# Reordered work at both ends of a 32-sequence graph-attention kernel: statistics, reciprocals, adds and a weight combination

## The chip, the cores and the metric

The kernel runs on one core of one Trainium2 chip. The metric is the device time of one execution in microseconds (us), as the median of several executions; before the change it is 3678.03 us (3 runs, 3677.95 to 3679.01; the profiled run took 3678.18). The profile takes one execution apart. In it PE is TensorE's matmuls, PEld its weight loads, DVE is VectorE, ACT ScalarE, POOL GpSimd and SP SyncE, which starts transfers. L389 is line 389 of the kernel that was profiled. A PSUM tile (psum.tile in the code) is a buffer into which matmuls write their results. "Half clock" is a stretch in which the profile gives TensorE's granted clock as 0.50, as from 217 to 223 us before the change. The change adds some ten lines, so one statement has different line numbers before and after; the tile names stay.

## The reference, cut to what matters

Two residual layers act on x of 32 sequences x 512 rows x 512 features, with one adjacency matrix of 512 x 512 for all.

```python
# layer 0: masked attention, 8 heads of 64
h = jnp.maximum(_layernorm(x), 0.0)
q, k, v = h @ Wq + bq, h @ Wk + bk, h @ Wv + bv          # split into heads
scores = q @ k.T / sqrt(64) + (1.0 - adj) * -1e9
x = x + (softmax(scores) @ v) @ Wo + bo
# layer 1: graph attention, one head
h = jnp.maximum(_layernorm(x), 0.0)
g = h @ W;  s1, s2 = g @ a1, g @ a2
e = leaky_relu(s1[:, None] + s2[None, :], 0.2) * adj
x = x + elu(softmax(e) @ g + beta * g)
```

## The kernel before

It runs in steps. Step b works on layer 0 of sequence b, on the output projection of sequence b-1 and on layer 1 of sequence b-2. Each step is a string of parts in the order in which they are issued. The instructions of one engine run in the order in which they are issued; engines wait for one another only where data demand it. Small VectorE jobs ("later") stand in queues: each is due after so many us of TensorE work, and is issued where the issuing code finds it due, or where somebody needs it. So a number in a table of due times decides an order on VectorE.

```python
GAP = (12.0, 14.0, 28.0, 24.0)                       # when the reciprocals of a head pair are due
GAPS = {0: (14.0, 1.0, 4.0, 24.0), 1: (12.0, 12.0, 2.0, 24.0)}
# ...
        for k in range(T):
            mask(k)                                  # additive mask of the scores, four tiles
            dve(1.9)
        for t in range(T):
            later("bad", 30.0, 200.0, 1.35, lambda t=t: other(t))   # is adj 0/1? tiles sq, bad
# ...
    def finish(b, j, st):                            # softmax denominators of one pair of heads
        need("rd")
        pd = psum.tile([P, N], F32, name=f"pd_{b}_{j}", tag="pd")
        # ... matmuls of the sums of e with ones into pd ...
        for k in range(2):                           # two reciprocals rd, then o * rd on GpSimd
            later("rd", 0.0, gap(b, (j + 1) % NP) + 3.0, 1.7, lambda k=k: divide(k))

    def residual(b, st, i, tag="x1", bufs=3):        # x + c_row, the start of the residual
        # ... load ...
            for t in range(n):
                nc.gpsimd.tensor_tensor(r[:, t, :], r[:, t, :], c_row, op=ALU.add)
# ...
    def final(b, t, st):                             # one output tile: matmuls py, then
        # ...
        nc.scalar.activation(y, p, AF.Exp, scale=r)
        nc.vector.tensor_scalar(y, y, 1.0, -1.0, op0=ALU.min, op1=ALU.add)
        nc.vector.scalar_tensor_tensor(y, p, r, y, op0=ALU.mult, op1=ALU.max)
        dve(1.9)
        nc.gpsimd.tensor_tensor(y, y, x1_of(st, t), op=ALU.add)
        nc.sync.dma_start(out[b, ts(t, P), :], y)
# ...
        def W():                                     # output projection of sequence b-1 ...
            need("wa")
            fourth(b - 1, "uT", prev["oT"])
            run(out_proj(b - 1, prev))               # ... whose last pieces queue statistics
            if b == B:
                run_all(("hn", b - 1))               # norm and the two dots of each row tile
# ...
        order = {
            0: "0.V1.NH2c.3wK.Q", 1: "0.VUrR1.W2.NH3K.Q", B - 1: "0.VDU1.rRG2.W3.t", B: "0yrR.zUWDGY",
            B + 1: "DGJY",
        }.get(b, "0.VDU1.G2.rYNRWH3.KQ")
# ...
        combine(nc.vector, wk, ak)                   # at the start: five combinations of wk's blocks
        turn(0, states[0])
        t1 = first_combo(0, "tT", states[0]["h"][0], nc.vector)     # the difference tT
```

The letters: a digit is the scores (matmuls ps, tiles e) of that head pair and the values (po) of the pair before; "." its denominators (pd); V, K, Q the projections of layer 0; r and R the two halves of the residual; U the combinations oT and uT of the attention's output; W the output projection; D the "diagonal" of layer 1 (row sums pe, then beta on the diagonal of the attention tiles at); G the matmuls pg; Y the output tiles (py, then y); y and z output tiles of sequence b-3. A projection is made in seven products of halves instead of eight; its PSUM tiles are x, qz and y, with the weight's letter behind (x_k, qz_q, y_w). Every sequence's dot products pass through DRAM as a row (s) before the tiles at can be made.

## Time and profile before

| what | value |
|---|---|
| time, median | 3678.03 us |
| span of the profiled execution | 3676.4 us |
| TensorE busy | 3606.2 us, 98% of the span |
| TensorE not busy | 70.2 us |
| its waits from 3520 us to the end | 34.8 us |
| its waits from 300 to 3450 us | 9.4 us in 28 pieces |

TensorE is the bound; what can be won is its idle time, and the slow matmuls behind long idle times. The three views to read are the busy line of the page, the list of what TensorE waited for, cut by time, and the timeline around each wait. The prediction shows the lines.

### The profile page before, as it was taken

What the parts mean: (1) busy time and instruction counts of PE and PEld (TensorE: products, weight loads), DVE (VectorE), ACT (ScalarE), POOL (GpSimd) and SP (SyncE); (2) the same over time, 40 slices, a digit from 0 to 9 for tenths busy, and PEclk for the clock granted to TensorE, in tenths of its full rate; (3) what the DMA queues carried; (4) which work ended last, traced back from release to release, by engine and by line L of the source; (5) the groups of instructions that cost most, each with busy time, mean ns of one, the idle gap of its engine ahead of it and who ended that gap; (6) DMA issues with size and microseconds to landing.
All of it is one profiled execution on the core that took longest, in us unless ns stands there. A gap on an engine that the chain in (4) does not pass through costs nothing. (4 is left out here: it accounts for less than half of the span.)

```text
span 3676.4 us, 58866 instructions
## 1 busy us (share of the span) xinstructions
PE 3606.2 (98%) x24310; PEld 1875.1 (51%) x24310; DVE 2802.5 (76%) x4119; ACT 1398.2 (38%) x2086; POOL 1147.1 (31%) x965
## 2 busy tenths in 40 slices
PE   9999999999999999999999999999999999999986
PEld 5545554555554555545555545555455555455532
DVE  6977777787777877777877778777778777787783
ACT  3433334334333433343333334333434343343331
POOL 5423333223333222332233332323332333323241
PEclk9999999999999999999999999999999999999998
DMA  3001111101111011111011110011110111100100
GB/s 130 18 7 35 38 38 35 33 9 38 38 38 35 10 32 38 38 35 38 4 38 38 38 35 14 28 38 38 35 38 4 38 38 38 35 18 24 32 27 27
DMA packets 71074, 120.58 MB, mean 33 GB/s; under 512 B 11856, under 2 KB 15952, under 8 KB 70800
## 3 DMA queue, kind: packets, MB, share of 16 engines
q1 hardware_dynamic: 69216, 114.91, 9.9%
q8 instruction: 193, 3.16, 0.4%
q10 hardware_dynamic: 1376, 1.57, 0.1%
q14 instruction: 81, 0.66, 0.1%
q0 software_dynamic: 208, 0.27, 0.0%
HBM read 83.11 MB, written 33.62 MB: 32 GB/s over the span
## 5 line engine op out<-in xcount | busy, mean ns | idle before, releaser
L620 POOL TENSOR_TENSOR oT<-oT,rd 128x512 f32<-128x512 f32 x128 | 167.2, 1306 | 1527.1 <-DVE rd L613 1524.5
L567 ACT ACTIVATE e<-e 128x1024 f32<-128x1024 f32 x512 | 541.0, 1057 | 196.0 <-DVE e L552 160.0
L552 DVE TENSOR_TENSOR e<-ps,nmT 128x1024 f32<-128x1024 f32 x384 | 455.1, 1213 | 101.9 <-PE ps L542 101.8
L542 PE MATMUL ps<-qT,kT 64*128 64x512 f32 x2048 | 483.4, 606 | 12.7 <-DVE e L552 12.7
L590 PE MATMUL po<-e,v 128*64 128x512 f32 x2048 | 463.1, 593 | 0.0
L51 PE MATMUL pg<-at,hn 128*64 128x512 f32 x2048 | 449.7, 598 | 13.2 <-DVE dmax L775 13.2
L51 PE MATMUL py<-w,gT 128*64 128x512 f32 x2048 | 447.4, 595 | 0.1
L613 DVE RECIPROCAL rd<-pd 128x256 f32<-128x256 f32 x256 | 435.0, 1729 | 0.0
L804 POOL TENSOR_TENSOR y<-y,x 128x512 f32<-128x512 f32 x128 | 193.2, 1509 | 544.9 <-DVE y L802 489.9
L542 PEld LDWEIGHTS ps<-qT,kT 64*128 64x128 f32 x2048 | 184.2, 186 | 309.4 <-issue 214.9
L564 DVE TENSOR_TENSOR es<-es,e 128x1024 f32<-128x1024 f32 x254 | 316.6, 1246 | 13.2 <-ACT e L567 0.6
L51 PEld LDWEIGHTS pg<-at,hn 128*64 128x64 f32 x2048 | 148.9, 138 | 307.5 <-issue 307.5
L51 PEld LDWEIGHTS py<-w,gT 128*64 128x64 f32 x2048 | 148.1, 138 | 293.9 <-issue 292.3
L590 PEld LDWEIGHTS po<-e,v 128*64 128x64 f32 x2048 | 157.8, 138 | 235.1 <-issue 225.4
L598 ACT COPY oT<-po 128x512 f32<-128x512 f32 x128 | 73.8, 576 | 388.2 <-PE po L590 388.2
L714 DVE CUSTOM_DVE_ANT_0 scr<-hn,wa_r 128x512 f32<-128x512 f32 x256 | 169.9, 719 | 49.0 <-ACT hn L701 49.0
L619 ACT ACTIVATE rj<-rd 128x512 bf16<-128x512 f32 x128 | 80.7, 630 | 327.5 <-DVE rd L613 327.4
L741 ACT ACTIVATE at<-at 128x512 f32<-128x512 f32 x128 | 80.4, 628 | 286.3 <-DVE at L737 286.3
L800 ACT ACTIVATE y<-py,rd 128x512 f32<-128x512 f32 x128 | 87.6, 685 | 261.2 <-PE py L51 253.0
L564 DVE TENSOR_TENSOR es<-e,e 128x1024 f32<-128x1024 f32 x127 | 180.9, 1424 | 0.7 <-PE pd L605 0.7
L639 POOL TENSOR_TENSOR x<-x,c_row 128x512 f32<-128x512 f32 x128 | 176.9, 1403 | 0.0
L321 POOL TENSOR_TENSOR rs<-rs,mhalf 128x2 f32<-128x2 f32 (+1 forms) x97 | 78.7, 811 | 306.9 <-DVE rs L320 305.8
(189 smaller groups left out, 5726.5 us busy)
## 6 DMA issues: line engine op xcount, KB each, us to landing
x<-in_x_dram SPq DMA_DIRECT2D x128, 256.0 KB, 3.0
out_dram<-y SPq DMA_DIRECT2D x128, 256.0 KB, 2.1
x<-in_x_dram SPq DMA_DIRECT2D x63, 512.0 KB, 4.2
s<-row_s SPq DMA_DIRECT2D x32, 256.0 KB, 4.2
adj<-in_adj_dram SPq DMA_DIRECT2D x4, 256.0 KB, 7.1
w<-in_L_gnn_W_dram SPq DMA_DIRECT2D x1, 1024.0 KB, 7.9
wk<-in_L_gnn_Wk_dram ACTq DMA_DIRECT2D x3, 256.0 KB, 8.9
wq<-in_L_gnn_Wq_dram SPq DMA_DIRECT2D x3, 256.0 KB, 7.6
```

The costliest lines, as they stand in the source:

```text
L51: nc.tensor.matmul(out[s : s + HD], lhsT[:, s : s + HD], rhs, start=start, stop=stop, skip_group_check=onto)
L542: nc.tensor.matmul(ps[s], st["kT"][j][rows, ts(k, P)], st["qT"][j][rows, :], start=True, stop=True)
L552: nc.vector.tensor_tensor(e, p, nmT[:, k, :].unsqueeze(1).to_broadcast([P, 2, N]), op=ALU.add)
L564: (nc.gpsimd if early else nc.vector).tensor_tensor(es, one, e, op=ALU.add)
L567: nc.scalar.activation(e, e, AF.Exp)
L590: nc.tensor.matmul(po[s * HD : (s + 1) * HD, :], v[k // 2][:, k % 2, (2 * j + s) * HD : (2 * j + s + 1) * HD], e[k][:, s, :], start=k == 0 ...
L613: nc.vector.reciprocal(rd[:, ts(k, H)], pd[:, ts(k, H)])
L620: nc.gpsimd.tensor_tensor(o, o, rd, op=ALU.mult)
L639: nc.gpsimd.tensor_tensor(r[:, t, :], r[:, t, :], c_row, op=ALU.add)
L714: nc.vector.tensor_tensor_reduce(scr, st["hn"][t], r, 1.0, 0.0, op0=ALU.mult, op1=ALU.add, accum_out=st["s12"][:, g, t : t + 1],)
L800: nc.scalar.activation(y, p, AF.Exp, scale=r)
L804: nc.gpsimd.tensor_tensor(y, y, x1_of(st, t), op=ALU.add)
```

## The change

Its intent is to shorten TensorE's waits at both ends, where there is no other sequence's work to fill them. Its parts: (1) only the first of wk's five combinations stays ahead of the difference tT, for which the second group of matmuls, qz_k, waits; (2) two masks are queued; (3) the adjacency checks (sq, bad) are due at 60 instead of 30; (4) the reciprocals of sequence 1's third pair are due at 14 instead of 24, and the last sequence gets due times of its own; (5) in the last step VectorE, not GpSimd, adds c_row to the residual and the residual to the outputs of sequence 30; (6) the statistics of sequence 31 come after the diagonal of sequence 30.

```diff
-GAPS = {0: (14.0, 1.0, 4.0, 24.0), 1: (12.0, 12.0, 2.0, 24.0)}
+GAPS = {0: (14.0, 1.0, 4.0, 24.0), 1: (12.0, 12.0, 2.0, 14.0)}
+LAST_GAPS = (3.0, 14.0, 12.0, 3.0)
 ...
         for k in range(T):
-            mask(k)
-            dve(1.9)
+            if k < 2:
+                mask(k)
+                dve(1.9)
+            else:
+                later("nm", 0.0, 5.0, 1.9, lambda k=k: mask(k))
         for t in range(T):
-            later("bad", 30.0, 200.0, 1.35, lambda t=t: other(t))
+            later("bad", 60.0, 200.0, 1.35, lambda t=t: other(t))
 ...                                   (combine is split into combine_first and combine_rest)
-        return GAPS.get(b, GAP)[j]
+        return (LAST_GAPS if b == B - 1 else GAPS.get(b, GAP))[j]
 ...
+        eng = nc.vector if b == B - 1 else nc.gpsimd
 ...
-                nc.gpsimd.tensor_tensor(r[:, t, :], r[:, t, :], c_row, op=ALU.add)
+                eng.tensor_tensor(r[:, t, :], r[:, t, :], c_row, op=ALU.add)
 ...
-        nc.gpsimd.tensor_tensor(y, y, x1_of(st, t), op=ALU.add)
+        (nc.vector if b == B - 2 else nc.gpsimd).tensor_tensor(y, y, x1_of(st, t), op=ALU.add)
 ...
-            if b == B:
-                run_all(("hn", b - 1))
 ...
-            "t": T1, "J": judge,
+            "t": T1, "n": lambda: run_all(("hn", b - 1)), "J": judge,
 ...
-            0: "0.V1.NH2c.3wK.Q", 1: "0.VUrR1.W2.NH3K.Q", B - 1: "0.VDU1.rRG2.W3.t", B: "0yrR.zUWDGY",
+            0: "0.V1.NH2c.3wK.Q", 1: "0.VUrR1.W2.NH3K.Q", B - 1: "0.VDU1.rRG2.W3.t", B: "0yrR.zUWDnGY",
 ...
-        combine(nc.vector, wk, ak)
+        combine_first(nc.vector, wk, ak)
         turn(0, states[0])
         t1 = first_combo(0, "tT", states[0]["h"][0], nc.vector)
+        combine_rest(nc.vector, wk, ak)
 ...
+        need("nm")
         for b in range(B + 2):
```

## The prediction

> **What bounds the kernel now.** I read the page first: TensorE is busy 98% of the span, at full clock in every slice, the last excepted.
>
> ```profile
> PE 3606.2 (98%) x24310; PEld 1875.1 (51%) x24310; DVE 2802.5 (76%) x4119; ACT 1398.2 (38%) x2086; POOL 1147.1 (31%) x965
> ...
> PE   9999999999999999999999999999999999999986
> ```
>
> So 70.2 us of the span (3676.4 - 3606.2) is all that a change which touches no matmul can win; part of it is mere issue time. The second view, TensorE's waits by window, says where they lie: from 400 to 3300 us only 8.7 us, in 26 pieces of at most 0.3. The middle is one long row of matmuls, so what the start gains reaches the end whole. From 3520 us on there are 34.8 us of waits; four of the six rows (what was waited for; us in total, times, longest):
>
> ```profile
> PE pg L51 <- DVE dmax L775: 13.2, 2, 11.1
> PE pe L51 <- DVE as L748: 10.6, 1, 10.6
> PE pd L605 <- DVE rd L613: 4.9, 1, 4.9
> PE y_w L51 <- POOL uT L379: 3.7, 1, 3.7
> ```
>
> The first 300 us hold some 16 us more. The third view, the timeline (start, duration, engine, line, operation, count, idle before), gives the three waits of the start that the change aims at:
>
> ```profile
> 18.51 0.69 DVE L373 TENSOR_TENSOR tT<-hT 128x512 f32<-128x512 f32 x1
> ...
> 19.34 1.95 PE L51 MATMUL qz_k<-tT,wk 128*64 128x256 f32 x16 [1.54 <-DVE tT L373]
> ...
> 81.62 1.13 PE L542 MATMUL ps<-qT,kT 64*128 64x512 f32 x4 [1.54 <-DVE e L552]
> ...
> 219.06 1.98 PE L605 MATMUL pd<-es,ones 128*64 128x512 f32 x4 [5.49 <-DVE rd L613]
> 220.82 3.03 PE L51 MATMUL x_v<-wv,hT 128*64 128x256 f32 x16
> 223.68 1.90 PE L51 MATMUL qz_v<-wv,hT 128*64 128x256 f32 x16
> ```
>
> The last three lines show a cost that no wait list has: after the idle 5.49 us the four pd take 1.98 us (1.08 elsewhere) and the 16 x_v 3.03 (1.90). From 219.06 to 223.68 is 4.62 us for 0.91 + 1.73 = 2.64 us of work, so 1.98 us is lost behind the wait. The waits of 4.86, 11.14 and 10.60 us at the end are followed by the same slow matmuls (for the second, 64 pg in 16.29 us against 13.90); those of 1.54 and 3.74 us are not.
>
> **What the skill says.** "TensorE: Matmul & The Clock Gate", section "What's actually happening", gives half clock after about 3.4 us of idleness and full clock after about 3.4 us of work. The trace agrees: the edge lies between 3.74 and 4.86 us, and a crossing loses 2.0 to 2.9 us. "SBUF — State Buffer", section "Who interferes with whom", says that GpSimd and a VectorE instruction with two SBUF inputs take an exclusive lock, one wholly blocking the other. The trace agrees: beside GpSimd's adds a dot product on VectorE takes 1.74 us, alone 0.69:
>
> ```profile
> 3551.67 6.29 POOL L639 TENSOR_TENSOR x<-x,c_row 128x512 f32<-128x512 f32 x4
> ...
> 3555.10 1.74 DVE L714 CUSTOM_DVE_ANT_0 scr<-hn,wa_r 128x512 f32<-128x512 f32 x1
> ...
> 3560.12 0.68 DVE L714 CUSTOM_DVE_ANT_0 scr<-hn,wa_r 128x512 f32<-128x512 f32 x1
> ```
>
> A 128x512 add costs GpSimd 1.27 us alone and up to 1.7 contended; VectorE 0.61 apart, and some 1.05 more for each GpSimd instruction it meets.
>
> **The change, part by part.** I compared the instruction order of both builds. TensorE's order is identical. The deferred masks move nothing on any engine: 0.
>
> *Split of wk.* The difference tT moves ahead of four of wk's five combinations. S1 starts at 15.63, tT runs 16.24 to 16.93, so qz_k is released before x_k is done (15.85 + 1.73 = 17.58) and starts at 17.6 instead of 19.34: **-1.7**. GpSimd's combinations of hT and wq follow tT and come forward too.
>
> *Adjacency checks later.* Two pairs (sq, bad), 4.6 us of VectorE from 75.77 to 80.35, leave the place ahead of e_2_0; its scores are ready near 78.3, so the wait of 1.54 at 81.62 goes. They come back: three such pairs now stand ahead of e_1_0 of sequence 1, where VectorE idled 0.92 us before. One pair more, partly contended, is 1.3 to 2.3 us; up to 1.1 of it can reach TensorE. Net **-0.7**.
>
> *Reciprocals of sequence 1 sooner.* rd_2 (two of 1.67) moves ahead of the query projection's combinations, as sequences from 2 on have it. Then pd at 219.06 waits for nothing: 5.49 and 1.98. The third es and the reciprocals displace the at-tiles, whose exp held up the qz_q copy on ScalarE: its wait of 0.83 at 201.10 goes as well. The at-sums end near 218 on the new clock, ahead of their diagonal near 226. **-8.3**.
>
> *The last step.* Here waits hang on one another, so I follow the new order with the durations of the old trace.
> - rd_2's second half follows y_0 directly: 3546.8 to 3548.5 instead of 3550.29 to 3552.04. So pd_3 starts at 3548.7, the wait shrinks from 4.86 to 1.4, and the clock stays up (-2.9 of its own).
> - py_2, py_3, x_w and qz_w then end at 3559.9. But y_w needs uT, which needs rd_3, and VectorE's row to rd_3 is: y_1 (held by rj_2 on ScalarE until 3550.0) 1.2, four c_row adds 3.5 (one contended), three dots 1.84, y_2 1.2, two dots 2.3 (one contended), y_3 1.2, rd_3 3.4: 3564.6, against 3566.67. GpSimd's product and uT take 3.3 more, as before. y_w starts at 3568.05, not 3570.15. TensorE waits 8.1 us there instead of 3.74 and loses the clock, some 2.4 us. What pd_3 won is nearly all handed on to this wait.
> - x_w then ends about where it did, 3574; the last qz_w starts at 3577.6 instead of 3579.93 and ends at 3579.5. The logits now come after it on VectorE: last statistics pair 1.8, x add 0.6, three at of 1.38, ScalarE's exp, last sum: pe starts at 3587.0, **later** than before (3581.82). But its diagonal no longer stands behind the other statistics and eight dots: pg starts 3.3 us after pe, 3590.3 against 3594.13: -3.8.
> - The half clock at the start of pg stays (16.1 us to py). py_0 starts at 3606.4. The four y adds of sequence 30 leave GpSimd, so the contended at instructions fall from 1.65 and 1.75 us to about 0.69:
>
> ```profile
> 3631.35 1.65 POOL L804 TENSOR_TENSOR y<-y,x 128x512 f32<-128x512 f32 x1 [3.96 <-DVE y L802]
> 3631.92 1.63 DVE L737 SCALAR_TENSOR_TENSOR at<-at 128x512 f32<-128x512 f32 x1
> ...
> 3635.09 1.23 PE L51 MATMUL pe<-ones,as 128*64 128x64 f32 x16 [10.60 <-DVE as L748]
> ```
>
> In the new order ScalarE and VectorE hand over y_1, y_2, at_2, y_3, at_3 one after the other: y_0's exp at 3610.1; y_1's at 3614.6; y_2's results on VectorE 3617.75 to 3619.6; at_2 to 3620.9; y_3's exp 3621.6, its three VectorE instructions to 3624.1; at_3 to 3625.5, exp to 3626.2, last sum 3626.9; pe at 3627.0. Before it was 3635.09: **-8.1** for the whole last step. The rest (diagonal, pg, py, output) keeps its 41 us.
>
> Sum: -1.7 - 0.7 - 8.3 - 8.1 = -18.8; 3678.0 - 18.8 = 3659.2, or 0.5%.
>
> **Rivals.** *Every named wait vanishes with its half clock* (34.8 of the end, 8.6 of the start and some 9 of clock): about 3626. The diff's intent speaks for it; against it stand the fixed orders of VectorE and ScalarE, where a removed wait meets the next producer. *The end gives nothing back*: VectorE takes on eight adds and the dots of sequence 30 finish only at about 3568, the row through DRAM takes 6 us (198.42 behind a dot that ended at 192.3), and the first at stands ahead of x_31's adds in the row. If row or contention cost 3 to 5 us more, the last qz_w waits and only the start remains: about 3667. For it speaks the late row; against it that x_w's half clock leaves until 3574.3 for it. *VectorE becomes the bound*: it has 76% busy and the change adds eight adds, 5 us; I see no place in the middle where the order changed.
>
> **Range and chances.** The start is firm to about 1.5 us, being direct waits with no successor near. The end is a chain of ten guesses with perhaps 5 us error, and the half clock may come or not at three places (2.4 us each). So **3659 us**, 3651 to 3667 in 8 of 10. 2% is 73.6 us, more than all the idle time: faster by over 2% 0.005, within 0.985, slower 0.01.
>
> **What would show it.** qz_k at 17.6; no wait of rd near 215 and pd at 1.08 us; pd_3 waiting some 1.4 us, y_w 8 us for uT and then slow matmuls; pe of sequence 30 waiting 7 us and pg 2 us after it, instead of 11; pe of sequence 31 waiting about 7 with no 1.6 us instruction ahead of it. I am wrong if y_w's wait is under 4 us (then the end gives more than I allow), or if qz_w or at_0 waits for the row.

## The result, and the profile after

The changed kernel takes 3661.43 us (4 runs, 3661.13 to 3661.78) beside 3677.99 us of the kernel before (4 runs, 3676.76 to 3679.01) on the same chip: 16.6 us less. The ratio is 0.9955, 95% interval 0.9938 to 0.9972. (A ratio is the mean time of one kernel's fast runs over that of the other's in the same rounds, so it is not quite the ratio of the medians that I quote.) The outputs are correct. The spans of the two profiles differ by 17.1 us (3676.4 and 3659.3), and I use those where I follow single instructions.

From the page of the kernel after, the busy line and TensorE's row of the span in 40 slices (tenths busy):

```profile
PE 3603.1 (98%) x24310; PEld 1873.9 (51%) x24310; DVE 2802.2 (77%) x4127; ACT 1398.4 (38%) x2086; POOL 1134.5 (31%) x957
...
PE   9999999999999999999999999999999999999997
```

The number of matmuls is the same. TensorE's busy time fell by 3.1 us net, for matmuls that no longer run at half clock. GpSimd has eight instructions less and VectorE eight more, yet VectorE's busy time did not grow: its other work met GpSimd less often. The other 14.0 of the 17.1 us (17.1 - 3.1) are idle time of TensorE that went. The list of what TensorE waited for from 3450 us on (us in total, times, longest):

```profile
PE pe L52 <- DVE nb L707: 8.1, 1, 8.1
PE pe L52 <- DVE as L759: 7.1, 1, 7.1
PE y_w L52 <- POOL uT L389: 6.4, 1, 6.4
PE pg L52 <- DVE dmax L784: 2.1, 1, 2.1
PE pg L52 <- DVE dmax L786: 2.1, 1, 2.1
PE pd L615 <- DVE rd L623: 1.4, 1, 1.4
PE x_w L52 <- DVE y L813: 1.2, 1, 1.2
```

28.4 us stand here where 34.8 stood. Of the four rows of before, that of pg went from 13.2 to 4.2, and pe came to 8.1 in its place; that of pd went from 4.9 to 1.4, and y_w rose from 3.7 to 6.4 in its place. That is the pattern to see: a removed wait came back for the most part at the next matmul that depends on the same queue. The timeline shows the start, where the gain is direct:

```profile
17.79 1.90 PE L52 MATMUL qz_k<-tT,wk 128*64 128x256 f32 x16
...
75.99 3.71 PE L552 MATMUL ps<-qT,kT 64*128 64x512 f32 x16
...
212.03 1.08 PE L615 MATMUL pd<-es,ones 128*64 128x512 f32 x4
212.94 1.90 PE L52 MATMUL x_v<-wv,hT 128*64 128x256 f32 x16
214.67 1.90 PE L52 MATMUL qz_v<-wv,hT 128*64 128x256 f32 x16
```

None of the lines has a bracket with an idle time: the waits of 1.54, 1.54 and 5.49 us are gone, and so are the slow pd and x_v. From the start of pd to that of qz_v it is 2.64 us instead of 4.62. Around the last step the dots and adds of VectorE, and GpSimd's row, look like this on the timeline:

```profile
3542.05 3.57 DVE L650 TENSOR_TENSOR x<-x,c_row 128x512 f32<-128x512 f32 x4
3545.54 0.68 DVE L725 CUSTOM_DVE_ANT_0 scr<-hn,wa_r 128x512 f32<-128x512 f32 x1
...
3549.17 1.76 DVE L725 CUSTOM_DVE_ANT_0 scr<-hn,wa_r 128x512 f32<-128x512 f32 x1
```

The four adds take VectorE 3.57 us where GpSimd needed 6.29, and the dots behind them run at 0.68 us. Of the eight dots of this stretch three still meet GpSimd and take 1.73 to 1.76 us (the one shown meets an output add of sequence 29); before it was six, at 1.53 to 1.75. The last two waits:

```profile
3615.69 0.69 DVE L748 SCALAR_TENSOR_TENSOR at<-at 128x512 f32<-128x512 f32 x1
...
3617.93 1.22 PE L52 MATMUL pe<-ones,as 128*64 128x64 f32 x16 [7.14 <-DVE as L759]
3621.23 16.55 PE L52 MATMUL pg<-at,hn 128*64 128x512 f32 x64 [2.08 <-DVE dmax L786]
```

The tile at takes 0.69 us instead of 1.63. pe of sequence 31 is 17.16 us earlier (3635.09 - 3617.93) and waits 7.14 instead of 10.60 us.

The shift of single instructions against the kernel before tells where the gain came:

| instruction | before, us | after, us | shift | gained since the line above |
|---|---|---|---|---|
| qz_k, sequence 0 | 19.34 | 17.79 | -1.55 | 1.55 |
| qz_q, sequence 0 | 45.50 | 44.26 | -1.24 | -0.31 |
| x_k, third use | 179.53 | 178.66 | -0.87 | -0.37 |
| ps, after the wait at pd | 241.75 | 232.65 | -9.10 | 8.23 |
| py_0 of sequence 29 | 3540.29 | 3531.15 | -9.14 | 0.04 |
| pg of sequence 30 | 3594.13 | 3580.47 | -13.66 | 4.52 |
| pe of sequence 31 | 3635.09 | 3617.93 | -17.16 | 3.50 |

The very first projection, x_k, started 0.16 us later after (16.01 for 15.85), since its loads landed later; counted from x_k, qz_k gained 1.71 us and qz_q kept 1.40 of them.

### The profile page after: what moved, and what is told of

It is laid out like the page before. It is cut to its first block, busy times and chain, and to the rows that moved or that the text cites.

```text
span 3659.3 us, 58865 instructions
## 1 busy us (share of the span) xinstructions
PE 3603.1 (98%) x24310; PEld 1873.9 (51%) x24310; DVE 2802.2 (77%) x4127; ACT 1398.4 (38%) x2086; POOL 1134.5 (31%) x957
## 5 line engine op out<-in xcount | busy, mean ns | idle before, releaser
L552 PE MATMUL ps<-qT,kT 64*128 64x512 f32 x2048 | 483.7, 606 | 12.8 <-DVE e L562 12.7
```

What stands on the lines that cost most here:

```text
L552: nc.tensor.matmul(ps[s], st["kT"][j][rows, ts(k, P)], st["qT"][j][rows, :], start=True, stop=True)
```

## The experiments

Twelve runs were made, eleven of other kernels and one of the changed kernel again, in three batches, each timed five times, with nine runs of the kernel before on the same chip in each batch (medians 3677.69, 3677.78 and 3677.72). All outputs were correct. Differences are to the changed kernel (3661.43; 3661.62 when it ran again).

One thing sets how fine these differences can be read. The first projection x_k starts when the first loads have landed, and in the fourteen profiles it started anywhere from 15.77 to 17.25 us, in the kernels whose start is identical too. Also the half clock after a long wait ends sooner or later from run to run: pg of sequence 30, whose waits and matmuls are the same in most of them, took 15.31 to 16.92 us. The last step as a whole, from py_0 of sequence 29 to pe of sequence 31, took 86.78 to 88.16 us in the five profiles in which it is unchanged (after, after_again, u_wk, u_bad, u_gaps); the profile "after" is the fastest of them. So I trust a difference of medians to about 1 us, and below that use the traces: each from its own x_k for the start, and single waits for the end.

### The masks: not run

Undoing part (2) alone gives, on all five engines, the same order of instructions as the changed kernel. A comparison of the two builds shows it, so there was nothing to run. The prediction's 0 stands by construction.

### u_wk: the split of wk undone

```diff
         combine_first(nc.vector, wk, ak)
+        combine_rest(nc.vector, wk, ak)
         turn(0, states[0])
         t1 = first_combo(0, "tT", states[0]["h"][0], nc.vector)
-        combine_rest(nc.vector, wk, ak)
```

> The changed kernel with wk's combinations put back ahead of the transposes; nothing else moves. Theory (the split is worth what reached the later start, 1.2 us, since 0.3 of the 1.55 us won at qz_k was given back to contended mask instructions): 3662.6 us, the wait of 1.5 us at qz_k back. Rival (the 1.7 us of the prediction): 3663.1. Rival (the masks hand it all back): 3661.4.

Measured: 3662.97 us (3661.97 to 3663.71), +1.5; ratio to the kernel before 0.996 (0.9946 to 0.9973). But its profile has no wait at qz_k. In that execution the block a_k of wk landed before the transposes of x were done: the first combination ran at 14.80, x_k at 16.96, and tT at 17.67, behind all five combinations, was still early enough for qz_k at 18.74. In the profile of the kernel before, the first combination ran only at 15.63, 0.22 us ahead of x_k. So what the split is worth depends on which load lands first. With a_k early it even costs: from x_k to the pd of sequence 1 (212.03 us in the kernel after) it is 195.48 us here and 196.02 in the changed kernel, and the wait for qT at qz_q is 0.99 us here and 1.51 there. The median does not speak for the split either. This profiled run is the median one, and its span is 1.8 us longer because x_k started 0.95 us later and the half clocks of the last step were 1.3 us longer, less these 0.54. On the split the run is inconclusive.

### u_bad: the adjacency checks at 30 again

```diff
-            later("bad", 60.0, 200.0, 1.35, lambda t=t: other(t))
+            later("bad", 30.0, 200.0, 1.35, lambda t=t: other(t))
```

> The changed kernel with the adjacency checks due 30 us after their listing again instead of 60. Theory (moving them cost more later, three small waits of 0.54, 0.54 and 0.16 us and 0.5 more at the fourth score tile, than the 1.54 us it removed): 0.4 us faster than the changed kernel, about 3661.0, the wait of 1.5 us near 80 us back and the waits near 125 and 146 us gone. Rival (the prediction: the move gains 0.7): 3662.1.

Measured: 3660.89 us (3660.74 to 3662.85), 0.5 less than with the move; ratio 0.9955. Counted from x_k, pd of 212.03 in the kernel after is at 196.02 us, and here at 195.18: without the move the start is 0.84 us **shorter**. The timeline of this run, then that of the changed kernel, in lines that waited:

```profile
81.35 1.13 PE L552 MATMUL ps<-qT,kT 64*128 64x512 f32 x4 [1.54 <-DVE e L562]
...
93.90 1.13 PE L552 MATMUL ps<-qT,kT 64*128 64x512 f32 x4 [0.75 <-DVE e L562]
```

```profile
92.04 1.13 PE L552 MATMUL ps<-qT,kT 64*128 64x512 f32 x4 [1.68 <-DVE e L562]
...
125.10 1.13 PE L552 MATMUL ps<-qT,kT 64*128 64x512 f32 x4 [0.54 <-DVE e L562]
...
146.07 1.13 PE L552 MATMUL ps<-qT,kT 64*128 64x512 f32 x4 [0.54 <-DVE e L562]
```

The move does take away 1.54 us at 81, and returns it in three places. At 92 the three sums es of VectorE run beside GpSimd's combinations of wo, which the move has shifted against them: they take 2.16 + 4.32 = 6.48 us instead of 1.23 + 4.32 = 5.55. At 125 a row-constant dot of 1.74 us (tile scr) now stands ahead of the tile e. At 146 three check pairs stand ahead of e instead of two. So this part costs 0.5 to 0.8 us. The prediction had the wrong sign.

### u_gaps: the reciprocals of sequence 1 at 24 again

```diff
-GAPS = {0: (14.0, 1.0, 4.0, 24.0), 1: (12.0, 12.0, 2.0, 14.0)}
+GAPS = {0: (14.0, 1.0, 4.0, 24.0), 1: (12.0, 12.0, 2.0, 24.0)}
```

> The changed kernel with sequence 1's last gap at 24 again. Theory: the wait for rd_2 comes back near 215 us with its half clock and the wait for the qz_q copy, 8.2 us: 3669.6. Rival (the middle has slack that takes up what the start loses): under 3664.

Measured: 3670.64 us (3670.35 to 3671.08), +9.2; ratio 0.9981 (0.9967 to 0.9994). Its timeline:

```profile
217.70 1.97 PE L615 MATMUL pd<-es,ones 128*64 128x512 f32 x4 [5.49 <-DVE rd L623]
219.46 3.62 PE L52 MATMUL x_v<-wv,hT 128*64 128x256 f32 x16
```

The wait of 5.49 us is back, and so is the half clock behind it (pd 1.97 for 1.08, x_v 3.62 for 1.90). By the trace the part is worth 8.5 us (62.53 and 53.99 from x_k of sequence 1 to the ps after pd); the other 0.7 of the medians is within the scatter. One number in a table is about half of the whole gain.

### u_hn: the last statistics ahead of the diagonal again

```diff
             run(out_proj(b - 1, prev))
+            if b == B:
+                run_all(("hn", b - 1))
```

> The changed kernel with the last statistics and dots ahead of the diagonal again. Theory (what counts at the end is when the last at sums are ready, not when pg of sequence 30 starts): pg of sequence 30 starts about 7.5 us later, near 3588, but the at tiles of sequence 31 are then done before its y tiles, so the diagonal of 31 follows py without its 7.1 us wait: total within 2 us of 3661.4. Rival (the 11 us wait is simply back): about 3668.9.

Measured: 3663.57 us (3662.71 to 3665.11), +2.1; ratio 0.9962. The timeline:

```profile
3586.20 1.22 PE L52 MATMUL pe<-ones,as 128*64 128x64 f32 x16 [16.32 <-DVE as L759]
...
3618.92 1.07 PE L52 MATMUL pe<-ones,as 128*64 128x64 f32 x16
3623.83 15.65 PE L52 MATMUL pg<-at,hn 128*64 128x512 f32 x64 [3.83 <-DVE dmax L786]
```

pe of sequence 30 waits 16.32 us instead of 8.12, so pg of sequence 30 comes 8.4 us later, counted from py_0 of sequence 29 (57.70 and 49.32 us). But the statistics of sequence 31 are then done early, its four tiles at are made while pg runs (3589.44 to 3595.1 on VectorE), and pe of sequence 31 follows py without any wait. All but 2.1 us are paid back, just outside the 2 us that the theory allowed. The rival, a loss handed through whole, is refuted. This run shows something else: with the tiles at of sequence 31 ahead of the tiles y, the wait of 7.14 us is not needed. The last experiments use that.

### u_yadd: the output adds of sequence 30 back on GpSimd

```diff
-        (nc.vector if b == B - 2 else nc.gpsimd).tensor_tensor(y, y, x1_of(st, t), op=ALU.add)
+        nc.gpsimd.tensor_tensor(y, y, x1_of(st, t), op=ALU.add)
```

> The changed kernel with the four y adds of sequence 30 on GpSimd again. Theory: each add meets one VectorE instruction with two SBUF inputs and stretches it by about 1 us (at second instruction 0.69 to 1.65), four times, while the four adds leave VectorE's chain (0.75 each): pe of sequence 31 about 1 us later, 3662.4. Rival (contention is the whole of the last wait's gain, 3.7 us): 3665.1. Rival (no contention on the chain): 3658.5.

Measured: 3662.72 us (3661.51 to 3663.99), +1.3; ratio 0.9959. Three of the four adds again run beside VectorE's at, which takes 1.63 to 1.65 us instead of 0.69; the fourth runs beside a tensor_scalar of y, which takes 1.33 instead of 0.43. From py of sequence 30 to pe of sequence 31 it is 22.17 us (3597.26 to 3619.43) instead of 21.19 (3596.74 to 3617.93): 1.0 us. In the kernel before it was 24.85. So 1.0 of the 3.66 us by which this stretch shrank is due to the engine of the adds. The other 2.7 I put down to the new order: at_0 now runs before the first y, where it followed it, and two of the tiles y follow each other with no tile at between them. u_last bears this out. Its adds are on VectorE too, but there at_0 comes only behind y_1, and the same stretch takes 24.28 us (3594.33 to 3618.61), 3.1 more than in the changed kernel.

### u_res: the c_row adds of the last residual back on GpSimd

```diff
-        eng = nc.vector if b == B - 1 else nc.gpsimd
+        eng = nc.gpsimd
```

> The changed kernel with the four c_row adds of sequence 31 on GpSimd again. Theory: VectorE loses 3.6 us of adds, but its dots then meet GpSimd's adds at 1.7 instead of 0.7 us, four to five of them; rd_3 ends within 1.5 us of 3555.3: 3661.4 to 3663. Rival (VectorE's four adds are a pure burden on the way to rd_3): 3 us faster, 3658.4.

Measured: 3663.39 us (3662.39 to 3664.53), +2.0; ratio 0.9961. y_w waits 7.70 us instead of 6.41, and its half clock lasts longer (3.68 us, then 2.67 for x_w, where 1.90 is normal). pe of sequence 31 is 0.9 us later than in the changed kernel, counted from py_0 of sequence 29. But up to pg of sequence 30 this run is 2.1 us behind (51.41 and 49.32 us from py_0): 1.0 of it are waits (1.29 more at y_w, 0.28 less at x_w), and the rest is the longer half clock, which differs by run; then pg happened to be 1.15 us shorter (15.31 and 16.46). So the waits give 1.0 and the medians 2.0, and the scatter of the half clock is as large as the difference.

### u_last: the last sequence's own due times removed

```diff
-        return (LAST_GAPS if b == B - 1 else GAPS.get(b, GAP))[j]
+        return GAPS.get(b, GAP)[j]
```

> The changed kernel without the gaps of the last step. Theory: rd_2's second half falls behind two dots and y_1 again, pd_3 waits about 4 us, but y_w's wait shrinks by nearly as much, since rd_3 is what VectorE's row allows: 1 to 4 us slower, 3662.5 to 3665.5. Rival (the sooner reciprocals are the larger part of the 8 us of the end): 3667 or more.

Measured: 3662.36 us (3660.97 to 3663.84), +0.9; ratio 0.9958. Rows from its list of TensorE's waits:

```profile
PE pe L52 <- DVE as L759: 10.4, 1, 10.4
PE pd L615 <- DVE rd L623: 8.3, 1, 8.3
PE y_w L52 <- POOL uT L389: 3.8, 1, 3.8
```

pd waits 8.3 us instead of 1.4, 7 us more, and all but 1 us comes back: y_w waits 2.6 us less, pe of sequence 30 does not wait at all, where it waited 8.12, and pg of sequence 30 is even 1.4 us earlier (3579.04). Then pe of sequence 31 waits 10.4. The total is just under the theory's range (3662.5 to 3665.5), the way is not as it had it: pd waited twice the 4 us expected, because the four c_row adds (3.55 us, now on VectorE) also stand ahead of rd_2's second half, and most of it came back at pe and not at y_w. That a wait of 7 us can be put in for 0.9 us is the plainest proof that the waits of the last step hand on to one another.

### b_rd: the reciprocals for y_w issued at once

```diff
-            ... B: "0yrR.zUWDnGY",
+            ... B: "0yrR.ezUWDnGY",        # "e": run_all("rd"), the last two reciprocals
```

> The changed kernel with rd_3 forced directly behind the c_row adds, ahead of y_2, y_3 and the dots. Theory (the wait at y_w is handed on; what holds the end is VectorE's row with its dots, the row through memory and the at tiles): y_w starts about 5 us sooner and keeps the clock, but pe of sequence 30 comes within 2 us of where it was and the total within 2 us of 3661.4. Rival (y_w's wait of 6.4 us and its half clock are on the path): about 3655.

Measured: 3662.05 us (3660.52 to 3662.53), +0.6; ratio 0.9956. From the timeline of this run:

```profile
3552.12 3.60 PE L52 MATMUL x_w<-wo,oT 128*64 128x256 f32 x16 [4.14 <-DVE y L813]
...
3558.38 1.95 PE L52 MATMUL y_w<-wo,uT 128*64 128x256 f32 x16 [0.90 <-POOL uT L389]
3560.16 1.90 PE L52 MATMUL x_w<-wo,oT 128*64 128x256 f32 x16
```

The wait at y_w, the third largest of the list, went from 6.41 to 0.90 us, and nothing was won. The wait moved to x_w, whose PSUM tile py_2 had filled and VectorE had not yet read out: its y_2 now stands behind the reciprocals. The half clock moved along (x_w 3.60 us). My figure for y_w itself was wrong: I had it come about 5 us sooner, and counted from py_0 it came 0.9 sooner. So the run does not test by itself whether 6.4 us less at y_w would be on the path. What it shows is that the output projection's last qz_w came 1.3 us sooner and pe of sequence 30 only 0.3, because VectorE's row set pe (it waited 9.13 us for VectorE); the total is as the theory had it.

### after_again: the changed kernel once more

> The changed kernel itself, beside the three that follow, so that all four are compared on one chip: 3661 to 3662.5 us (3661.43 in its first runs). Every theory expects that; it shows what the scatter of the first tile's landing does.

Measured: 3661.62 us (3661.0 to 3663.54); ratio 0.9957. It repeats the first result within 0.2 us, with one run of five 2 us higher. It is the base of the next three.

### b_at: the last tiles at ahead of the tiles y

```diff
-            ... B: "0yrR.zUWDnGY",
+            ... B: "0yrR.zUWDnGAY",        # "A": run_all(("at", b - 1))
```

> The attention tiles of sequence 31 are made before the output tiles y of sequence 30, so that pe(31) can follow py directly. Theory (TensorE waits 7.1 us there only because VectorE does the y tiles first): the wait at pe(31) is gone and pe(31) runs some 7 us sooner; the diagonal products of 31 still wait for y_3 and d_max, but now with a wait of about 4 us at pg(31), so of the 7.1 us some 3.5 to 4 come back, or all of the 7.1 if that short wait keeps full clock: 3654 to 3658. Rival (VectorE's total of y and attention work sets the end, in whatever order): pg(31) where it was, 3660 to 3662.

Measured: 3656.15 us (3654.64 to 3656.54), -5.5; ratio 0.994 (0.9927 to 0.9954). Its timeline:

```profile
3612.67 1.07 PE L52 MATMUL pe<-ones,as 128*64 128x64 f32 x16
3617.57 15.65 PE L52 MATMUL pg<-at,hn 128*64 128x512 f32 x64 [3.83 <-DVE dmax L786]
```

pe of sequence 31 follows py directly, and pg of sequence 31 waits 3.83 us for the diagonal behind y_3; the clock drops there (15.65 us instead of 13.9). The theory holds: the wait of 7.14 us was an order on VectorE, not a lack of VectorE time. The rival is out.

### b_diag: the last diagonal among the tiles y as well

```diff
-        pd = psum.tile([P, T, HD], F32, name=f"pe_{b}", tag="x")
+        pd = psum.tile([P, T, HD], F32, name=f"pe_{b}", tag="pd" if b == B - 1 else "x")
 ...
-            ... B: "0yrR.zUWDnGY",   B + 1: "DGJY",
+            ... B: "0yrR.zUWDnGAfdl", B + 1: "GJY",   # f: Y((0, 1)), d: diagonal(31), l: Y((2, 3))
```

> As the run before, and the diagonal's VectorE work of sequence 31 stands between the first two and the last two y tiles, with a PSUM tile of its own. Theory: pe(31) and pg(31) follow py without a wait and at full clock: 7.1 + 2.1 of waits and some 2.6 us of half clock (pg(31) 16.55 instead of 13.9) go, 11 to 12 us, less 1 us if y_3 then ends late: 3649 to 3651. Rival (the y tiles moved behind come to end the span, or pg(31) waits all the same): 3654 or more.

Measured: 3649.74 us (3648.72 to 3650.24), -11.9; ratio 0.9924 (0.991 to 0.9937). The timeline of its end:

```profile
3598.20 7.05 PE L52 MATMUL py<-w,gT 128*64 128x512 f32 x32
3605.07 1.07 PE L52 MATMUL pe<-ones,as 128*64 128x64 f32 x16
3605.95 7.05 PE L52 MATMUL py<-w,gT 128*64 128x512 f32 x32
3612.82 13.91 PE L52 MATMUL pg<-at,hn 128*64 128x512 f32 x64
```

No line has a bracket: TensorE runs from py to the last matmul without a wait, and pg takes 13.91 us, full clock throughout. From the first py to the last group of py it is 28.59 us (3598.20 to 3626.79) instead of 41.09 (3596.74 to 3637.83). Order and PSUM tag were changed together; no run parts them.

### b_diag_bad: the same, with the adjacency checks at 30

> As the run before, and the adjacency checks are due at 30 again, as in the kernel before. Theory (the later checks cost 0.4 to 0.8 us, where the prediction had a gain of 0.7): 0.4 to 0.8 below the run before it, near the scatter of such runs. Rival (the prediction's sign was right): 0.7 above it.

The edit is that of b_diag and that of u_bad together. Measured: 3648.91 us (3648.60 to 3649.46), 0.83 below b_diag on the same chip; ratio to the kernel before 0.9922 (0.9908 to 0.9935). Counted from x_k, pd of sequence 1 is at 195.22 us here (211.56 - 16.34) and at 196.02 in b_diag (212.86 - 16.84), so the sign of u_bad repeats: the moved checks cost 0.8 us. This is the fastest kernel, 28.8 us below the kernel before and 12.7 below the changed one on the same chip (3661.62 - 3648.91).

## Why the prediction was right or wrong

The prediction had 3659.2 us by its sum, 18.8 us of gain; measured are 3661.43 us and 16.6 (17.1 by the spans). The time lies inside its range of 3651 to 3667 and, as it said, within 2% of the kernel before. Term by term, with the shifts of the table in "The result":

| term | predicted | in the traces | what the run with the part undone says |
|---|---|---|---|
| later landing of x_k | 0 | +0.16 | scatter |
| split of wk | -1.7 | -1.40 | cost 0.5 with a_k early; with a_k late not run |
| adjacency checks later | -0.7 | +0.37 | +0.5 to +0.8 |
| reciprocals of sequence 1 | -8.3 | -8.23 | -9.2 by the medians, -8.5 by the trace |
| last step | -8.1 | -8.02 | -0.9 to -2.1 for each of four parts |
| deferred masks | 0 | 0 | the same order on every engine |
| sum | -18.8 | -17.12 | |

**Reciprocals: right, and for the stated reason.** The wait of 5.49 us and the slow matmuls behind it went, and nothing came in their place. The prediction read the half clock as part of the wait's price, and u_gaps shows it so.

**Last step: right in its steps, and the close sum is partly luck.** It followed the new order of VectorE row by row with old durations. Put on its own clock (9.14 us, the shift at py_0, added to the times after), its marks and the trace are: pd_3 3548.7 and 3548.71; y_w 3568.05 and 3567.93; last qz_w 3577.6 and 3576.28; pe of sequence 30 3587.0 and 3586.30; pg 3590.3 and 3589.61; pe of sequence 31 3627.0 and 3627.07. Its idea, that what pd_3 won is handed on to y_w and comes out only at pg and pe, is what u_last confirms in kind: there 7 us put in at pd_3 came back, for the most part at pe of sequence 30. The luck: from py_0 to pe it was 94.80 us before, and the five profiles with this last step gave 86.78 to 88.16, so the gain is 6.6 to 8.0 us by execution, and 8.02 is its upper end. The half clock at y_w, "some 2.4" us, cost 1.44 in this profile (y_w 3.34 for 1.90); u_res lost 2.55 there (3.68 and 2.67, less twice 1.90), so it differs by run and the figure was fair. One detail failed: x_w waits 1.19 us for y_2 to leave its PSUM tile, which the prediction did not have ("py_2, py_3, x_w and qz_w then end at 3559.9"). It cost nothing, because y_w waits behind it anyhow; its wait was predicted as 8.1 us, and 6.41 + 1.19 is 7.6.

**Adjacency checks: wrong, and this is the mis-sized term of the sum.** The step that failed is "One pair more, partly contended, is 1.3 to 2.3 us; up to 1.1 of it can reach TensorE. Net **-0.7**." The wait at 81 went, and the extra pair ahead of e_1_0 cost 0.54 us, which is within that sentence. What it lacked are two effects further away: GpSimd's wo combinations now met the sums es (6.48 us instead of 6.01 in the kernel before, and the next wait 1.68 instead of 1.21), and a row-constant dot came to stand ahead of the tile e at 125 us (0.54). Moving a job in a shared queue also moves everything that is queued behind it, and its phase to GpSimd. These waits (0.47 + 0.54 + 0.54, and 0.16 at 158) make 1.71 against the 1.54 that was removed; the last 0.2 of the shift of 0.37 I did not find.

**Split of wk: right in kind, 0.3 too large.** qz_k came at 17.79 without a wait, for the predicted 17.6; counted from x_k the gain there is the predicted 1.7. Then 0.3 was lost again: the query projection's wait for qT grew from 1.15 to 1.51 us. In an execution in which a_k lands early there is nothing to win, as u_wk's profile shows, so this term has a spread that the prediction did not give it.

**Rivals.** "Every named wait vanishes" is refuted by the 28.4 us that stand in the list after. "The end gives nothing back" is refuted by 8.02 us there. VectorE is no bound: 76% became 77%. The prediction's tests (pd without a wait, pe of sequence 30 about 7 us and pg 2 us) came out as 0, 8.12 and 2.08, and neither of its signs of being wrong appeared (y_w waited 6.41 us, more than 4; neither qz_w nor at_0 of sequence 30 waited for the row). Two of its readings are slightly off without effect: the listed waits of the first 300 us come to 14.8 us and not "some 16", and from rd_3's end to y_w it was 3.48 us before, not 3.3.

One reading the prediction did not make was worth more than the error: the 7 us before the last pe, which it accepted as given, was an order on VectorE that could be changed. b_diag got 11.9 us from it.

## What to carry to other kernels

When an engine drains at the end of a program, do not add up the waits in the list: follow the order on the engine that releases them, because a wait removed there is usually paid at the next release (7 us put in cost 0.9, and 5.5 us taken out at one matmul came back at others and won nothing). The price of a wait that is long enough to drop TensorE's clock includes the slow matmuls after it, so look at the durations behind the bracket too. And to move a small job out of a busy place, check what else moves in its queue and against GpSimd; here that turned 0.7 us of expected gain into a loss.

## What the Trainium skill lacked or had wrong

- "TensorE: Matmul & The Clock Gate", section "What's actually happening": it puts the drop to half clock at about 3.4 us of idleness in a free-running window. The runs agree: a wait of 3.74 us kept full clock (y_w 1.95 us, kernel before), and waits of 3.79 us (y_w 2.80 us, u_last) and 3.83 us (pg 15.65 us for 13.91, b_at and u_hn) lost it; four waits cannot tell an edge from the phase of such a window. What the section does not say is that the drop can come after the wait: in u_last the granted clock was 1.00 in the first 0.9 us of y_w (3564.1 to 3565.0) and 0.50 from about 3565.1 to 3568.5. And one drop cost 1.4 to 3.0 us for the same matmuls (pg of sequence 30 took 15.31 to 16.92 us, 13.91 at full clock); the page reckons such a cost for another kernel only.
- "SBUF — State Buffer", section "Who interferes with whom": it has the exclusive lock between GpSimd and VectorE instructions with two SBUF inputs, and the runs agree, but it gives no size for short instructions. A 128x512 instruction on VectorE took 0.68 us alone and 1.63 to 1.76 beside GpSimd; a tensor_scalar, which the section counts among those that can contend, 0.43 and 1.33 to 1.49. Beside the same instructions of GpSimd in another phase, three sums of VectorE took 5.55, 6.01 and 6.48 us (u_bad, before, after).
- I read no page that says how much the landing of a kernel's first loads scatters. The first projection started between 15.77 and 17.25 us in fourteen profiles, which is as much as the smaller parts of such a change are worth.
